# Modulation's products in other forms: whole squares of weights ahead of block 0, the condition as small operand later

## The chip, the core and the metric

The kernel runs on one core of a Trainium2 chip. The metric is the device time of one execution in microseconds (us), the median of several runs. A core has a matrix engine (TensorE, here PE, with its weight loads listed as PEld), three engines for elementwise work (VectorE or DVE, ScalarE or ACT, GpSimd or POOL) and SyncE (SP), whose queue issues nearly all of this kernel's transfers. Each engine takes its instructions strictly in the order of the program. Engines wait for each other by semaphores. SBUF is the memory on the core, with 128 partitions. PSUM holds the results of matrix products.

A matrix product takes two operands. The stationary one is loaded first (a LDWEIGHTS, with as many columns as the result has partitions). The moving one streams through it; its columns are the columns of the result. For each float32 product that the program writes the trace has two records of load and product, for a transpose one.

## The reference

One transformer block whose normalizations are modulated by a condition. x has 8 batches of 1024 tokens of 512 features, the condition 8 rows of 512:

```python
mod = jax.nn.silu(condition) @ Wada + bada
sh_a, sc_a, gt_a, sh_m, sc_m, gt_m = jnp.split(mod, 6, axis=1)
xn = _layernorm(x, g1, be1)
xm = xn * (1.0 + sc_a[:, None, :]) + sh_a[:, None, :]
x = x + gt_a[:, None, :] * _attention(xm, Wqkv, Wproj, bproj)
xn = _layernorm(x, g2, be2)
xm = xn * (1.0 + sc_m[:, None, :]) + sh_m[:, None, :]
h = jax.nn.gelu(xm @ W1 + b1, approximate=False)
x = x + gt_m[:, None, :] * (h @ W2 + b2)
```

Attention has 16 heads of 32 features and is causal. Everything is float32. The change is about the first line: the condition's product with Wada, 8 rows by 512 by 3072, in six parts of 512 columns. Parts 0 and 1 (shift and gain of attention), 3 and 4 (shift and gain of the MLP) are made by `modulation(i)`, parts 2 and 5 by `gates`.

## The kernel before, in words

**Blocks.** The tokens are cut into 16 blocks of 512 (two for each batch). For each block the kernel projects K, Q and V, computes the scores and their softmax in 4 groups of 4 heads, projects out, and runs the MLP. The linear products use a scheme with seven products of quarters in place of eight (`strassen`, which makes `product("A11", "B11")`, then S2·T2, A12·B21, S1·T1, S3·T3, and as a tail S4·B22 and A22·T4). It needs sums of quarters of the weights (S1 to S4; `weight_sums`, line 826, on POOL, at the start for k, q, v of block 0) and differences of quarters of the activations (T1 to T4; lines 784, 786 and `either`, lines 167 and 170).

**Weights.** All weights come through a ring of 8 buffers of 256 KB, "w". `fetch` (lines 358 to 362) issues the load of the next piece on SP as soon as the program has released the buffer that it needs. A matrix of 512 by 512 is read as four quarters of 256 by 256 columns; `RAW` gives their order, (0,0), (1,0), (0,1), (1,1): first the half of the rows, then the half of the columns.

**Order of work.** The instruction streams are written by a planner in the program itself. It keeps a clock for each engine (`now`), books a duration for each instruction (`note`, `note_pe`), and knows when each buffer is written and free (`written`, `left`). The linear work is a list of steps, `plan`, run as a generator that yields whenever something else could go first. Plan -1, ahead of attention, is: modulation 0 and 1, the sums for K, the columns `norm_columns_a` (lines 488 to 491: gain and shift from modT), the transposes of block 0 ("at": line 764, then the modulated activations xm_a, lines 768 and 774), K, Q and V of block 0. While it runs, `alone[0]` is True. Then `alone[0]` becomes False, and plan 0 runs beside the attention of block 0: the preparation of W1 and W2 ("preps"), K of block 1, the gates of attention, Q, modulation 3, the transposes of block 1, V, modulation 4, the MLP's columns, the gates of the MLP. Beside attention, the planner at each step takes the thread whose booked wait is shortest, and picks DVE, ACT or POOL for a copy or a sum by its booked clocks (`sooner`, `either`, `copy_out`). So a booked duration at one place can move instructions at all later places.

**The preparation.** `preparation` (lines 847 and 170 or 167, with the stores of line 816) loads every quarter of W1 and W2 into a stage, replaces them in place by S1 to S4, and stores these to memory, from where later steps load them. Its loads and stores are issued on SP, between the loads of weights.

**The products that are changed.** `cond_act` is the condition after silu, 8 rows; four transposes on PE (line 445) and a copy (line 447) turn it into `condT`, 128 partitions by 4 pieces of 8 columns. `modulation(i)` takes four quarters of Wada. For each of 4 pieces c of the result and each of 4 pieces k of the sum it calls the helper `matmul` (lines 212 to 223), which makes four products, each with 32 columns of the weights as stationary operand and the 8 columns of condT as moving one (line 217): 64 products for one modulation. Result: 128 partitions (features) by 4 by 8, in a PSUM bank. `combine_out` (line 208) adds bada's columns into `modT`. `gates` (line 520) uses condT as the stationary operand instead (8 columns) and 256 columns of Wada as the moving one.

Of the kernel before, what the change touches and what calls it, by code (L numbers as in the profile page):

```python
# [9 lines left out]
F32 = mybir.dt.float32  # L10
# [12 lines left out]
def kernel(  # L23
# [33 lines left out]
    nc = tc.nc  # L57
    B, T, D = x.shape
    HD = W1.shape[1]
    P = 128  # L60
    hd = D // H
    scale = float(hd) ** -0.5
    TB = 512
    NTT = TB // P
    NHALF = T // TB
    NC = D // P
    NF = HD // P
    HPG = P // hd
    NMOD = 6 * NC
    NQ = HD // D  # L70
    HB = D // 2
    RING = 8

    const = ctx.enter_context(tc.tile_pool(name="const", bufs=1))
# [6 lines left out]
    tmp = ctx.enter_context(tc.tile_pool(name="tmp", bufs=2))  # L81
# [18 lines left out]
    COLUMN = 0.84  # L100
# [4 lines left out]
    def due(reads=(), writes=()):  # L105
        t = 0.0
        for k in reads:
            t = max(t, written.get(k, 0.0))
        for k in writes:
            t = max(t, left.get(k, 0.0))  # L110
        return t

    def note(engine, ns, reads=(), writes=(), port=False):
        start = max(now[engine], due(reads, writes))
        if port:
            start = max([start] + [b for a, b in pool_spans if a <= start < b])
        end = start + ns
        now[engine] = end
        if engine == "POOL":
            pool_spans.append((start, end))  # L120
            del pool_spans[:-16]
        for k in reads:
            left[k] = max(left.get(k, 0.0), end + SYNC)
        for k in writes:
            written[k] = end + SYNC
        return end
# [9 lines left out]
    def note_pe(ns, form, reads=(), writes=()):  # L136
        now["PE"] = max(now["PE"], due(reads, writes))
        if shape[0] != form:
            shape[0] = form
            now["PE"] += SWITCH  # L140
        note("PE", ns, reads)
        spent[0] += ns
        for k in writes:
            written[k] = now["PE"] + PIPE

    def note_act(ns, func, reads=(), writes=()):
        if func is not None and table[0] != func:
            table[0] = func
            ns += TABLE
        note("ACT", ns, reads, writes)  # L150

    def sooner(reads, writes, dve, act):

        t = due(reads, writes)
        return "DVE" if max(now["DVE"], t) + dve <= max(now["ACT"], t) + act else "ACT"
# [18 lines left out]
    banks = [ps_l.tile([P, TB], F32, tag=f"l{i}", name=f"bank_{i}") for i in range(3)]  # L174
    live = [False] * len(banks)
    BANK = "a bank"
# [5 lines left out]
    def lin_bank():  # L182
        i = min(
            (i for i in range(3) if not live[i]),
            key=lambda i: left.get(("l", i), 0.0),
        )
        live[i] = True
        return i

    def copy_out(dst, bank, src, writes=(), last=True):  # L190

        key = ("l", bank)
        if sooner([key], writes, 690, 585) == "DVE":
            nc.vector.tensor_copy(dst, src)
            note("DVE", 690, [key], writes)
        else:
            nc.scalar.copy(dst, src)
            note_act(585, None, [key], writes)
        live[bank] = not last
# [12 lines left out]
    def matmul(ps, lhsT, rhs, start, stop, reads=(), bank=None):  # L212

        for j in range(HPG):
            r = slice(j * hd, (j + 1) * hd)
            columns = lhsT[:, r] if len(lhsT.shape) == 2 else lhsT[:, j, :]
            nc.tensor.matmul(  # L217
                ps[r, :], columns, rhs, start=start, stop=stop, skip_group_check=True
            )
        n = 1  # L220
        for d in rhs.shape[1:]:
            n *= d
        note_pe(2 * COLUMN * n, "columns", reads, [] if bank is None else [("l", bank)])
# [30 lines left out]
    for w in range(1, NB):  # L254
# [11 lines left out]
        else:  # L266
# [10 lines left out]
            at = [("at", w + 2)] if w + 2 < NB else []  # L277
# [25 lines left out]
    RAW = ((0, 0), (1, 0), (0, 1), (1, 1))  # L303
# [43 lines left out]
    def fetch():  # L347

        while len(ring) < len(order) and (len(ring) < RING or len(ring) - RING in used):
            i = len(ring)  # L350
            at = order[i]
            is_sum = isinstance(at[2], str)
            if is_sum and (id(at[0]), *at[1:]) not in kept_sums:
                return
            w = wp.tile([P, D], F32, tag="w", name=f"w_{i}")
            note_dma(680, [], [("w", i)], freed.get(i - RING, 0.0) + 300)
            if len(at) == 4:
                nc.sync.dma_start(w.rearrange("p (k n) -> p k n", n=HB), quarter(*at))
            elif is_sum:
                nc.sync.dma_start(w, kept_sums[id(at[0]), at[1], at[2]])  # L360
            else:
                nc.sync.dma_start(w, rows_of(*at))
            ring.append(w)

    def take(count):
        i = taken[0]
        taken[0] += count
        return list(range(i, taken[0]))
# [6 lines left out]
    def release(*indices):  # L375
        used.update(indices)
        for i in indices:
            freed.setdefault(i, now["PE"])
        fetch()
# [10 lines left out]
    at, r0 = [], 0  # L390
# [29 lines left out]
    ident = const.tile([P, P], F32, tag="ident", name="ident")  # L420
# [4 lines left out]
    nc.gpsimd.memset(eps, EPS)  # L425
    ones = const.tile([P, hd], F32, tag="ones", name="ones")
    nc.gpsimd.memset(ones, 1.0)
    minus_half = const.tile([P, NTT], F32, tag="minus_half", name="minus_half")
    nc.gpsimd.memset(minus_half, -0.5)
    minus_ones = const.tile([P, P], BF16, tag="minus_ones", name="minus_ones")  # L430
# [12 lines left out]
    pc = banks[0][:, : NC * B].rearrange("p (c b) -> p c b", b=B)  # L443
    for c in range(NC):
        nc.tensor.transpose(pc[:, c, :], cond_act[:, ts(c, P)], ident[:B, :B])
    condT = const.tile([P, NC, B], F32, tag="condT", name="condT")
    nc.vector.tensor_copy(condT, pc)
    pcols = banks[1][:, :n_rows]
    nc.tensor.transpose(pcols, rows, ident[:n_rows, :n_rows])
    cols = const.tile([P, n_rows], F32, tag="cols", name="cols")  # L450
    nc.vector.tensor_copy(cols, pcols)
    modT = const.tile([P, NMOD, B], F32, tag="modT", name="modT")

    def modulation(i):
        at = take(4)
        fetch()
        if len(ring) <= at[-1]:
            yield [tail_key[0]], []
        part = {kf: halves(j) for kf, j in zip(RAW, at)}
        yield [("w", i) for i in at], [BANK]  # L460
        bank = lin_bank()
        pm = banks[bank][:, : NC * B].rearrange("p (c b) -> p c b", b=B)
        for c in range(NC):
            for k in range(NC):
                w = part[k // 2, c // 2][:, k % 2, ts(c % 2, P)]
                matmul(pm[:, c, :], w, condT[:, k, :], k == 0, k == NC - 1, [("w", i) for i in at], bank)
                note("PE", 90)
                yield [], []
        release(*at)
        combine_out(  # L470
            modT[:, ts(i, NC), :],
            bank,
            pm,
            cols[:, O_BADA + i * NC : O_BADA + (i + 1) * NC].unsqueeze(2).to_broadcast([P, NC, B]),
        )

    def half(i, size):
        return slice(i * size, (i + 1) * size)
# [104 lines left out]
    alone = [True]  # L583
# [1410 lines left out]
```

## Time and profile before

| | |
|---|---|
| median of 3 runs | 3505.04 us (3502.97 to 3507.28) |
| the profiled execution, its own time | 3510.74 us |
| its span, first to last instruction | 3509.0 us |
| PE busy | 3454.3 us, 98% |
| DVE, POOL, ACT busy | 2198.9, 2084.2, 1212.4 us |
| DMA, mean rate over the span | 140 GB/s |
| granted TensorE clock | 0.998 |

A row of the timeline has the start, the duration, the engine, the line, the operation, result<-operands, shapes and a count of merged instructions. In brackets stands how long the engine had been idle before, and what ended that; "issue" means that the profile shows nothing that the engine waited for. SPq is the queue of SP: a row of it is the issue of a transfer, not the transfer. The view by windows gives each engine's busy time and number of instructions in a stretch, then the granted clock, the mean busy share of the 16 DMA engines and the rate. The view of groups gives count | busy us, mean ns | idle us before. The view of waits gives who waited <- for whom: us in total, times, the longest.

### The profile page before, as it was taken

The page shows a single profiled execution, that of the slowest core. Times are in us where ns is not written, and L with a number is a line of the kernel's source. Part 1 is how long each engine was busy: PE and PEld are TensorE (multiplying, and loading weights), DVE is VectorE, ACT ScalarE, POOL GpSimd, SP SyncE. Part 2 cuts the span into 40 slices and gives each one's busy share as a digit, 9 for nine tenths or more (in the row PEclk, how much of TensorE's full clock was granted, in tenths as well). Part 3 has the DMA queues.
Part 4 walks back from the last instruction along what each step waited for, and adds up shares of the span by engine and source line. Part 5 has one row for each costly group of instructions (what it writes and reads, how often), then busy time and mean ns, then how long its engine had stood idle before and what let it go on. Part 6 is the DMA issues. An engine that isn't in the chain of part 4 may idle for free.

```text
span 3509.0 us, 120365 instructions
## 1 busy us (share of the span) xinstructions
PE 3454.3 (98%) x54429; PEld 1724.0 (49%) x54429; DVE 2198.9 (63%) x2401; ACT 1212.4 (35%) x1276; POOL 2084.2 (59%) x2258
## 2 busy tenths in 40 slices
PE   8999999999999999999999999999999999999999
PEld 4444445445554545445454454544555444554445
DVE  5766676564666656665666566765666756656563
ACT  2335333342233423335223342333423343232531
POOL 3767846666366663756727576275753658537660
PEclk9999999999999999999999999999999999999999
DMA  6843444535545445363454534545354544443334
GB/s 212 263 137 104 137 115 140 142 107 159 142 125 156 119 147 153 119 170 115 137 157 130 155 117 144 150 137 148 116 155 137 165 122 146 128 136 101 96 121 140
DMA packets 328194, 491.10 MB, mean 140 GB/s; under 512 B 27260, under 2 KB 177596, under 8 KB 324100
## 3 DMA queue, kind: packets, MB, share of 16 engines
q1 hardware_dynamic: 327568, 483.39, 47.1%
q8 instruction: 428, 7.01, 0.8%
q14 instruction: 82, 0.67, 0.1%
q10 hardware_dynamic: 116, 0.03, 0.0%
HBM read 425.57 MB, written 55.64 MB: 137 GB/s over the span
## 4 chain that ended last, share of the span: by engine, by line
PE 83%; POOL 7%; DMA 3%; DVE 3%; ACT 1%; issue 1%; SPq 1%; ACTq 0%; DVEq 0%; POOLq 0%
PE bank L217 59%; PE sc L1595 8%; PE st L1686 6%; PE po L1726 6%; POOL pT L1816 4%; PE st L1674 2%; PE bank L1747 2%; DMA hat_m<-held_m 1%; DVE mx L1610 1%; POOL hT L170 1%; ACT pT L1698 1%; DMA held_m<-xm_m 1%; PE bank L1648 0%; POOL xr L170 0%; DMA w<-in_L_cond_Wqkv_dram 0%
## 5 line engine op out<-in xcount | busy, mean ns | idle before, releaser
L1816 POOL TENSOR_TENSOR pT<-pT,pT 128x256 f32<-128x256 f32 (+3 forms) x1254 | 1219.7, 1007 | 298.5 <-PE po L1726 181.6
L1698 ACT ACTIVATE pT<-st 128x2048 f32<-128x2048 f32 x288 | 540.9, 1878 | 1065.1 <-PE st L1686 959.8
L217 PE MATMUL bank<-w,hT 128*32 128x256 f32 x14336 | 823.7, 380 | 0.4 <-issue 0.4
L1610 DVE TENSOR_REDUCE mx<-sc 128x4 f32<-128x2048 f32 (+3 forms) x384 | 665.9, 1755 | 235.6 <-PE sc L1595 229.5
L217 PEld LDWEIGHTS bank<-w,hT 128*32 128x32 f32 x14336 | 446.7, 110 | 390.3 <-issue 105.8
L217 PE MATMUL bank<-xm_m,w 128*32 128x256 f32 x8192 | 498.6, 381 | 3.6 <-ACT xm_m L774 2.2
L217 PE MATMUL bank<-t_m,w 128*32 128x256 f32 x6144 | 382.4, 380 | 0.9 <-DVE t_m L786 0.6
L217 PEld LDWEIGHTS bank<-xm_m,w 128*32 128x32 f32 x8192 | 255.6, 110 | 231.2 <-issue 62.2
L1703 POOL TENSOR_SCALAR_AFFINE_SELECT pT<-pT 128x512 f32<-128x512 f32 x256 | 167.5, 672 | 331.9 <-ACT pT L1698 329.4
L1607 DVE TENSOR_TENSOR sc<-sc,mask 128x1024 f32<-128x1024 f32 (+1 forms) x160 | 162.8, 1018 | 293.3 <-PE sc L1595 237.8
L1595 PE MATMUL sc<-kT,qT 32*128 32x512 f32 (+3 forms) x3072 | 329.5, 521 | 4.3 <-ACT pT L1698 3.3
L1726 PE MATMUL po<-pT,v 128*32 128x512 f32 (+3 forms) x3048 | 301.6, 490 | 3.9 <-POOL pT L1703 3.9
L1686 PE MATMUL st<-qT,kT 32*128 32x512 f32 (+3 forms) x3072 | 300.8, 487 | 0.0
L217 PEld LDWEIGHTS bank<-t_m,w 128*32 128x32 f32 x6144 | 189.6, 110 | 172.9 <-issue 48.5
L1765 DVE RECIPROCAL rec<-rec 128x128 f32<-128x128 f32 x256 | 227.3, 922 | 48.2 <-ACT rec L1756 48.2
L217 PE MATMUL bank<-xm_a,w 128*32 128x256 f32 x3968 | 243.4, 382 | 0.4 <-DMA w<-in_L_cond_Wqkv_dram 0.4
L217 PE MATMUL bank<-w,qT 128*32 128x512 f32 x2048 | 237.0, 595 | 1.1 <-DMA w<-in_L_cond_Wproj_dram 0.7
L1595 PEld LDWEIGHTS sc<-kT,qT 32*128 32x128 f32 x3072 | 129.6, 183 | 188.2 <-issue 88.4
L208 DVE TENSOR_TENSOR hT<-bank,u_u 128x512 f32<-128x512 f32 x187 | 126.6, 686 | 105.8 <-PE bank L217 103.1
L217 PE MATMUL bank<-t_a,w 128*32 128x256 f32 x2944 | 183.2, 380 | 0.0
L217 PEld LDWEIGHTS bank<-xm_a,w 128*32 128x32 f32 x3968 | 123.5, 110 | 110.3 <-issue 29.3
L1115 ACT ACTIVATE hT<-hT,cols 128x512 f32<-128x512 f32 x256 | 164.7, 712 | 35.9 <-DVE hT L208 28.5
(243 smaller groups left out, 3404.0 us busy)
## 6 DMA issues: line engine op xcount, KB each, us to landing
w<-in_L_cond_W_dram SPq DMA_DIRECT2D x384, 256.0 KB
w<-kept_up_S SPq DMA_DIRECT2D x256, 256.0 KB
w<-kept_down_S SPq DMA_DIRECT2D x256, 256.0 KB
w<-kept_qkv_S SPq DMA_DIRECT2D x180, 256.0 KB
w<-in_L_cond_Wqkv_dram SPq DMA_DIRECT2D x147, 256.0 KB
hat_a<-in_x_dram SPq DMA_DIRECT2D x64, 256.0 KB
xr<-in_x_dram SPq DMA_DIRECT2D x32, 512.0 KB
w<-in_L_cond_Wproj_dram SPq DMA_DIRECT2D x64, 256.0 KB
```

Of the source, the lines that this page charges most:

```text
L208: nc.vector.tensor_tensor(out, src, other, op)
L217: nc.tensor.matmul(ps[r, :], columns, rhs, start=start, stop=stop, skip_group_check=True)
L1115: nc.scalar.activation(hT[:, i, :], hT[:, i, :], AF.Gelu, bias=cols[:, O_B1 + f : O_B1 + f + 1])
L1595: nc.tensor.matmul(sc[:, j, c0 : c0 + w], qTs[n][r, gg, ts(qt, P)], keys_of(n, kh)[r, gg, :w], start=True, stop=True, skip_group_check=True,)
L1607: nc.vector.tensor_tensor(place, place, shape_of.to_broadcast(place.shape), ALU.add)
L1610: nc.vector.tensor_reduce(maxima[n, gg][:, kh, qt, :], sc[:, :, c0 : c0 + w], axis=AX.X, op=ALU.max)
L1686: nc.tensor.matmul(st[:, j, c0 : c0 + w], kT[r, gg, ts(k % NTT, P)], qT[r, gg, TB - w :], start=False, stop=True, skip_group_check=True,)
L1698: nc.scalar.activation(pT[:, :, :used], st[:, :, :used], AF.Exp, scale=scale)
L1703: nc.gpsimd.affine_select(diagonal, diagonal, pattern=[[0, HPG], [1, P]], compare_op=ALU.is_ge, fill=0.0, base=0, channel_multiplier=-1,)
L1726: nc.tensor.matmul(po[r, TB - w :], v[:, k % NTT, g * P + j * hd : g * P + (j + 1) * hd], pT[:, j, c0 : c0 + w], start=(k == 0), stop=last ...
L1765: nc.vector.reciprocal(some, some)
L1816: nc.gpsimd.tensor_tensor(into, into, pT[:, j, c0 : c0 + w], ALU.add)
```

## The change

Three things. First, `condT` becomes the first 8 columns of each 32-column piece of `cond_cols`, whose other columns are zero, and POOL makes a matrix `folded` at the start: four identity matrices of 32 by 32 under one another. Second, while `alone[0]` is True (modulation 0 and 1), a product takes a whole square of 128 by 128 weights as stationary operand and 8 columns of condT as moving one: 16 products in place of 64. They go quarter by quarter in the order in which the quarters are loaded, and each quarter's buffer is released right after its four products. Third, beside attention (modulation 3 and 4), `cond_cols` (32 columns) is the stationary operand and 256 columns of weights move. The four pieces k of the sum go to four different groups of 32 partitions of one bank, 8 products. A copy brings the bank to SBUF (`parts`, a tile of the tag "y"), and four products with `folded` add the four groups and turn the result so that features are on partitions, as before. The planner books 220 ns for each whole product, and 430 ns for each half of the columns in the third case; before it booked 103 ns for each of 16 calls. `modT` gets 20 pieces in place of 24; the last four were never written.

```diff
+    folded = const.tile([P, hd], F32, tag="folded", name="folded")
+    for j in range(HPG):
+        nc.gpsimd.tensor_copy(folded[j * hd : (j + 1) * hd, :], ident[j * hd : (j + 1) * hd, j * hd : (j + 1) * hd])
...
-    condT = const.tile([P, NC, B], F32, tag="condT", name="condT")
+    cond_cols = const.tile([P, NC, hd], F32, tag="condT", name="condT")
+    nc.gpsimd.memset(cond_cols, 0.0)
+    condT = cond_cols[:, :, :B]
     nc.vector.tensor_copy(condT, pc)
...
-    modT = const.tile([P, NMOD, B], F32, tag="modT", name="modT")
+    modT = const.tile([P, 5 * NC, B], F32, tag="modT", name="modT")
...
         bank = lin_bank()
+        if not alone[0]:
+            for fh in range(2):
+                for k in range(NC):
+                    nc.tensor.matmul(
+                        banks[bank][ts(k, hd), half(fh, HB)], cond_cols[:, k, :], part[k // 2, fh][:, k % 2, :],
+                        start=True, stop=True, skip_group_check=True,
+                    )
+                note_pe(2 * COLUMN * HB, "columns", [], [("l", bank)])
+            release(*at)
+            parts = tmp.tile([P, TB], F32, tag="y", name=f"mod_{i}")
+            copy_out(parts, bank, banks[bank], [("mod", i)])
+            yield [("mod", i)], [BANK]
+            bank = lin_bank()
         pm = banks[bank][:, : NC * B].rearrange("p (c b) -> p c b", b=B)
-        for c in range(NC):
-            for k in range(NC):
-                w = part[k // 2, c // 2][:, k % 2, ts(c % 2, P)]
-                matmul(pm[:, c, :], w, condT[:, k, :], k == 0, k == NC - 1, [("w", i) for i in at], bank)
-                note("PE", 90)
-                yield [], []
-        release(*at)
+        if not alone[0]:
+            for c in range(NC):
+                nc.tensor.matmul(
+                    pm[:, c, :], parts[:, ts(c, P)], folded[:, :B], start=c == 0, stop=True, skip_group_check=True,
+                )
+                note_pe(220, "whole", [("mod", i)], [("l", bank)])
+        for j, (kh, fh) in enumerate(RAW if alone[0] else ()):
+            for c in range(2 * fh, 2 * fh + 2):
+                for k in range(2 * kh, 2 * kh + 2):
+                    nc.tensor.matmul(
+                        pm[:, c, :], part[kh, fh][:, k % 2, ts(c % 2, P)], condT[:, k, :],
+                        start=j + c + k == 0, stop=k == NC - 1, skip_group_check=True,
+                    )
+                    note_pe(220, "whole", [("w", at[j])], [("l", bank)])
+                    yield [], []
+            release(at[j])
```

## The prediction

> **What bounds the kernel now.** I read the page first: busy times, queues, the chain that ended last.
>
> ```profile
> PE 3454.3 (98%) x54429; PEld 1724.0 (49%) x54429; DVE 2198.9 (63%) x2401; ACT 1212.4 (35%) x1276; POOL 2084.2 (59%) x2258
> ...
> q8 instruction: 428, 7.01, 0.8%
> ...
> PE 83%; POOL 7%; DMA 3%; DVE 3%; ACT 1%; issue 1%; SPq 1%; ACTq 0%; DVEq 0%; POOLq 0%
> ```
>
> TensorE is busy for 3454.3 of 3509.0 us and holds 83% of the chain. Only two things can move the time: PE's own work, and the 55 us in which PE stands. So the second view is the busy time by windows, cut at the places that the change touches (columns: us, PE, PEld, DVE, ACT, POOL, clock, DMA share, GB/s).
>
> ```profile
> 0.00:24.20 24.20, 9.71 (x281) 8.16 (x281) 9.64 (x23) 6.66 (x9) 6.45 (x17) 1.00 0.76 234
> 24.20:100.00 75.80, 75.80 (x1221) 41.00 (x1224) 51.85 (x67) 21.39 (x25) 32.15 (x41) 1.00 0.65 204
> 100.00:150.00 50.00, 45.12 (x896) 24.39 (x888) 37.09 (x46) 13.35 (x15) 35.57 (x50) 1.00 0.91 281
> 150.00:1000.00 850.00, 834.71 (x12864) 407.24 (x12868) 548.89 (x587) 303.25 (x316) 525.63 (x584) 1.00 0.46 135
> 1000.00:3509.00 2509.00, 2488.90 (x39184) 1243.18 (x39176) 1551.46 (x1680) 867.72 (x913) 1484.38 (x1569) 1.00 0.47 136
> ```
>
> PE stands 14.5 us before 24.2, never from there to 100, 4.9 us from 100 to 150, and 35.4 us in the 3359 us after. The change works in the first stretch (modulation 0 and 1) and the third (modulation 3 and 4). In the third, DMA is the nearly full resource. The third view is PE's timeline at the start.
>
> ```profile
> 13.55 1.15 PE L217 MATMUL bank<-condT,w 128*32 128x8 f32 x64 [0.27 <-DMA w<-in_L_cond_Wada_dram]
> 15.05 0.30 PE L217 MATMUL bank<-condT,w 128*32 128x8 f32 x8 [0.35 <-DMA w<-in_L_cond_Wada_dram]
> ...
> 18.42 0.72 PE L217 MATMUL bank<-condT,w 128*32 128x8 f32 x40 [3.07 <-issue]
> 19.07 2.82 PE L764 MATMUL bank<-ident,hat_a 128*128 128x128 f32 x12
> 23.13 1.12 PE L764 MATMUL bank<-ident,hat_a 128*128 128x128 f32 x4 [1.24 <-ACT xm_a L774]
> 24.18 3.03 PE L217 MATMUL bank<-xm_a,w 128*32 128x256 f32 x32
> 27.03 1.90 PE L217 MATMUL bank<-t_a,sums_k 128*32 128x256 f32 x32
> 35.67 1.91 PE L217 MATMUL bank<-t_a,w 128*32 128x256 f32 x32
> ```
>
> The last quarter of Wada is there at 15.05. Then PE stops 3.07 us in the middle of modulation 1, with weights and condition present and no releaser but "issue".
>
> **The change, part by part.**
>
> *The stall at 15.35.* PE had run 221 records by then:
>
> ```profile
> 0.00:15.40 15.40, 5.17 (x221) 1.00 0.80 246
> ```
>
> Queue q8 moves 428 packets of 7.01 MB, 16.4 kB each; PE issues twice 54429 records (loads and products), so 254 instructions to a packet. It is PE's instruction stream, and 221 records are 442 instructions, near two packets. I read the stall as a packet that came late. Modulation 0 and 1 now are 256 records; afterwards they are 16 products each, of two records, 64 in all. Then 221 records are reached only some 136 records past the 16 transposes, in the K projection, some 7 us after its start, when the packet has had twice the time. The stall goes.
>
> The Trainium skill, "Runtime: NRT & Kernel Launch", section "Instruction fetch mechanics", speaks against this: instructions come in 16 KiB blocks of 256 that the sequencer fetches itself while it executes, and the cost of a boundary is mostly hidden. The packet size agrees with 254 here, "hidden" does not agree with 3.07 us; if it held, the stall would be something else and stay (rival three).
>
> *The products themselves.* Whole squares load 128 columns each. The nearest row in that cold first stretch is the transposing of the condition, 128 columns loaded, 8 moved:
>
> ```profile
> 6.52 0.56 PE L445 MATMUL bank<-ident,cond_act 8*128 8x8 f32 x4 [6.52 <-ACT cond_act L439]
> ```
>
> Less the 0.24 of the last one's tail that is 0.107 us a record, 0.86 for the 8 records of a quarter. This is more PE time than now (3.4 us a modulation against 2.3, twice the 1.15 of the row of 13.55), but beside the landing of Wada. Quarters now go in the order they land: the second of modulation 1 starts at about 13.7, the last ends at about 16.3. So modT is ready near 16.5. After it stand four small DVE operations:
>
> ```profile
> 19.20 0.19 DVE L208 TENSOR_TENSOR modT<-bank,cols 128x32 f32<-128x32 f32 x1 [6.13 <-PE bank L217]
> ...
> 19.64 1.22 DVE L489 TENSOR_TENSOR gaina<-onepa,cols 128x32 f32<-128x32 f32 x1
> ...
> 21.00 1.21 DVE L491 TENSOR_TENSOR shifta<-shifta,modT 128x32 f32<-128x32 f32 x1
> ```
>
> Two of them took 1.2 us while POOL worked from 19.55 on; at 16.7 POOL still waits for weights (row below), so I take 0.2 to 0.4 each, done near 17.8 instead of 22.2. What is late next: PE's transposes, 12 in 2.6 us from 16.4 and 4 in 0.85, so the first K product at about 20.0 instead of 24.18, its length 2.85 as now. The second product needs POOL's second sum, the seventh of K needs POOL's t_a after eight sums:
>
> ```profile
> 19.55 1.26 POOL L826 TENSOR_TENSOR sums_k<-w,w 128x512 f32<-128x512 f32 x1 [16.93 <-DMA w<-in_L_cond_Wqkv_dram]
> 20.89 1.26 POOL L826 TENSOR_TENSOR sums_k<-sums_k,w 128x512 f32<-128x512 f32 x1
> ...
> 30.86 1.27 POOL L170 TENSOR_TENSOR t_a<-t_a,xm_a 128x512 f32<-128x512 f32 x1
> ```
>
> The sums start when Wqkv lands, behind Wada in the same DMA queue; that stays. Second sum at 22.15, second product at 22.9 instead of 27.03; seventh at 22.9 + 5 x 1.73 = 31.5, but t_a ends at 32.1, so 32.2 instead of 35.67. **Lead at 36 us: 3.5 us** (bounds: 0 if the stall stays; 4.1 if POOL does not hold the seventh). The four added POOL copies and the memset lie in the 17 us in which POOL waits for Wqkv; without that cover they would cost under 1 us. PE has no gap until 100, so the lead arrives there whole.
>
> *Modulation 3 and 4.*
>
> ```profile
> L217 PE MATMUL bank<-condT,w 128*32 128x8 f32 x256 | 3.2, 178 | 0.0
> ```
>
> They go: 3.2 us. They are replaced by 16 products of 256 columns, at the 1.73 us that 16 such products take (27.03 to 28.76 in the K projection: 32 records), 8 whole products of two records at 0.107 at most, 1.7 us (half at the full clock), and two more changes of form and back. That is 2.6 to 3.8, so -0.6 to +0.6; I take 0. The copy between the two steps is ACT's and PE does other products meanwhile (two sums of scores, two linear products in the new order). The tile that it fills is one of the two "y" buffers, free since the gate row's store, and b_out for gates m waits for the last matrix product on SP; behind it there stand weights that PE, by its order, reaches over 15 us of products later.
>
> *What moves.* The planner books other durations (16 times 220 ns for 16 times 103 at the start), so from the first V product on its choices differ: in the new instruction order PE has 1955 changes of form against 1965, and SP, from its 48th row on, another order of the preparation's loads. A change of form costs no more than the tail of a product, 0.18 us (1.91 busy, 1.73 step); a third of it, ten times, is -0.6 us. SP's order counts more, because of the third stretch:
>
> ```profile
> 119.00:150.00 31.00, 26.90 (x512) 14.23 (x504) 22.17 (x28) 8.47 (x8) 21.78 (x33) 1.00 0.99 293
> ...
> 115.24 3.32 SPq L847 DMA_DIRECT2D prep_down<-in_L_cond_W_dram  x4
> ...
> 139.46 0.39 SPq L358 DMA_DIRECT2D w<-in_L_cond_Wada_dram  x1
> 143.03 0.34 SPq L816 DMA_DIRECT2D kept_up_S<-prep_up  x1
> 144.11 1.59 SPq L358 DMA_DIRECT2D w<-in_L_cond_Wqkv_dram  x2
> ...
> 150.47 1.03 PE L520 MATMUL bank<-w,condT 128*8 128x256 f32 x4 [1.95 <-DMA w<-in_L_cond_Wada_dram]
> 151.91 0.85 PE L217 MATMUL bank<-xm_a,w 128*32 128x256 f32 x12 [0.41 <-DMA w<-in_L_cond_Wqkv_dram]
> ```
>
> DMA is 99% busy at 293 GB/s, and PE waits for the last quarter of Wada and for Wqkv. Counted along SP's order in transfers of 256 KB, that last quarter is the 128th now and the 134th afterwards: the store of 143.03 and four loads of prep_down stand ahead of it, and one more transfer earlier. Six transfers are 1.57 MB, at 293 GB/s 5.4 us. The full stretch begins when PE frees weight buffers and sums are done, so I let it begin earlier by the lead: 5.4 - 3.5 = **+1.9 us** when PE goes on, at about 152.4. PE comes there 3.5 us early and waits some 7 us: the lead is spent. Bounds: +5.4 if the stretch begins no earlier; -3.5 if the four loads of prep_up that SP now issues after 91 us, and in the new order ahead of two weights of Q, fill its earlier gap and make up for all. Soon after that SP's count is the same within two transfers in both orders, and DMA's share falls to 0.46 (window from 150).
>
> *The sum.* +1.9 - 0.6 = +1.3 us. The profiled execution took 3510.74 (span 3509.0 and 1.7 around it), 5.7 over the median of 3505.04; it would take 3512.0. Carried to the median: **3506 us**.
>
> **The rest of the run.** All later work is the same, in another order. Where PE stands after 150 us:
>
> ```profile
> PE st L1674 <- DVE mx L1610: 7.8, 8, 2.4
> PE po L1726 <- POOL pT L1703: 3.9, 5, 1.7
> PE bank L764 <- ACT hat_m L687: 3.5, 3, 2.7
> PE bank L1648 <- POOL mcols L1632: 3.3, 4, 1.3
> ```
>
> Twenty waits in these four groups, the longest of each in the last column, each a near miss of two engines. A new order deals them anew. Independent, they scatter by about 6 us; I centre that on zero and put it into the range.
>
> **Rivals.** *One, faster:* the lead is kept (the preparation, ahead by one load, leaves room) and the dealt waits fall by 5: 3505 - 3.5 - 5 = 3496. For it: a gap of SP that the load now fills.
>
> ```profile
> 82.50 0.83 SPq L360 DMA_DIRECT2D w<-kept_qkv_S  x2
> 91.08 0.32 SPq L816 DMA_DIRECT2D kept_up_S<-prep_up  x1
> ```
>
> SP issued nothing from 83.3 to 91.1. Against: the count of transfers in the full stretch.
>
> *Two, slower:* the store that now is issued at 143.03 waits for a sum of the preparation, and in the new order the last quarter of Wada stands behind it and four loads (0.83 us each, by the row of 115.24). If that sum comes no earlier, Wada is issued at 143.03 + 0.34 + 3.3 + 0.3 = 147.0 instead of 139.46, all of the third stretch ends 7.5 us later: 3512.5, over 0.2% above. It decides if the fourth sum is done later than 139 us; nothing in the order says by how much it moved up.
>
> *Three, the change does not do what it says:* the stall at the start was no late packet, or it comes again in the K projection. Then no lead, and the six transfers cost up to 5.4: 3505 to 3510, middle 3508.
>
> **How the numbers follow.** Forecast (lead spent, waits even; own range 3500 to 3512) 0.5; rival one 0.17; two 0.25; three 0.08. Each measured to about 0.2%, 7 us, which is what a measurement can tell from no change: of the forecast I count 0.03 as faster and 0.05 as slower by the scatter, of rival two 0.05 as same, of three 0.02 as slower. Faster 0.20, same 0.53, slower 0.27. The range reaches from rival one to rival two with the scatter of the waits behind it: 3494 to 3520.
>
> **What would show it.** Right: no "issue" gap near 15 us, modT of modulation 1 near 16.5, first K product near 20, the seventh waiting for POOL's t_a; then PE waiting 5 to 8 us at the last gates product before 155 us. Wrong: a stall of 3 us inside the K projection; the last Wada in time with PE still 3 us ahead at 160; or waits after 160 us that differ from 35 us by more than 8.

## The result, and the profile after

| | before | after |
|---|---|---|
| median of 7 runs beside each other | 3507.28 us (3502.97 to 3516.64) | 3519.81 us (3515.49 to 3522.39) |
| ratio, after to before | | 1.003, interval 1.002 to 1.004 |
| the profiled execution, its own time | 3510.74 us | 3519.79 us |
| its span | 3509.0 us | 3517.9 us |

The change costs about 10 us (7 to 14 by the interval), 0.3%. The forecast was 3506, no difference to be measured, with 3520 as the upper end of its range. So the time lies just inside the range, and the sign is that of rival two, to which with the others I gave 0.27.

First the page of the kernel after: busy times, shares of the chain that ended last.

```profile
PE 3462.8 (98%) x54029; PEld 1733.8 (49%) x54029; DVE 2218.3 (63%) x2426; ACT 1213.1 (34%) x1272; POOL 2087.2 (59%) x2249
...
PE 86%; POOL 4%; DVE 4%; DMA 3%; ACT 1%; issue 1%; SPq 0%; ACTq 0%; DVEq 0%; POOLq 0%
```

PE has 400 records fewer and is busy for 8.5 us longer. Fewer instructions were not less work. Then the view by windows, cut as in the prediction.

```profile
0.00:24.20 24.20, 16.21 (x77) 16.02 (x78) 6.62 (x21) 5.21 (x7) 7.83 (x22) 1.00 0.67 211
24.20:100.00 75.80, 75.80 (x1199) 40.37 (x1201) 51.05 (x68) 21.26 (x27) 31.02 (x37) 1.00 0.68 216
100.00:150.00 50.00, 44.27 (x704) 23.74 (x700) 38.30 (x46) 16.02 (x17) 34.58 (x50) 0.98 0.84 264
150.00:1000.00 850.00, 835.74 (x12832) 408.63 (x12836) 551.32 (x587) 303.95 (x317) 527.96 (x582) 1.00 0.45 135
1000.00:3509.00 2509.00, 2485.88 (x39152) 1242.59 (x39148) 1567.03 (x1697) 866.65 (x905) 1485.79 (x1559) 1.00 0.46 136
```

Up to 24.2 us PE is busy for 16.21 us (9.71 before) and yet gets through 77 records in place of 281. From 100 to 150 the granted clock is 0.98 and DMA is less full than before (0.84, was 0.91). PE's timeline shows the start:

```profile
8.89 13.79 PE L490 MATMUL bank<-condT,w 128*128 128x8 f32 x64 [1.30 <-DMA w<-in_L_cond_Wada_dram]
...
26.28 2.78 PE L217 MATMUL bank<-xm_a,w 128*32 128x256 f32 x32
```

The issue gap of 3.07 us is gone, and so are the waits for Wada's quarters, but the 64 records now last 13.79 us, 0.213 us each, without a pause. The first K product starts at 26.28: 2.1 us later than before (24.18), not 4.2 earlier. Now the third stretch. The rows of L470 and L483 are the new forms, the others its waits and what follows them:

```profile
108.99 1.05 PE L470 MATMUL bank<-w,condT 128*32 128x256 f32 x16
...
114.63 1.06 PE L483 MATMUL bank<-folded,mod 128*128 128x8 f32 x8
...
123.17 1.93 PE L217 MATMUL bank<-w,t_a 128*32 128x256 f32 x32 [1.67 <-DMA w<-kept_qkv_S]
...
144.21 1.06 PE L483 MATMUL bank<-folded,mod 128*128 128x8 f32 x8
...
149.81 2.09 PE L1622 MATMUL sc<-kT,qT 32*128 32x512 f32 x8 [3.38 <-DVE mx L1637]
151.82 4.63 PE L547 MATMUL bank<-w,condT 128*8 128x256 f32 x15
156.08 0.42 PE L217 MATMUL bank<-xm_a,w 128*32 128x256 f32 x3
```

No row here waits for Wada. PE waits 1.67 us for weights of V and 3.38 us for DVE's reduction of the scores, and right after that the 15 records of the gates take 4.63 us. The clock in that place, by windows:

```profile
147.50:154.30 6.80, 4.50 (x14) 1.30 (x15) 4.24 (x5) 2.93 (x4) 4.83 (x9) 0.50 1.08 334
```

For 6.8 us the granted clock is 0.50; PE is busy for 4.50 of them, so up to half of that, 2.25 us, is lost (an estimate). PE reaches the first product of block 1 with xm_a at 156.08, before at 151.91. For the remainder, one window from 160 us to the end in both kernels, before and then after:

```profile
160.00:3600.00 3440.00, 3314.49 (x51916) 1645.95 (x51904) 2093.00 (x2257) 1165.65 (x1222) 2006.82 (x2150) 1.00 0.46 132
```

```profile
160.00:3600.00 3440.00, 3316.48 (x51984) 1649.76 (x51976) 2115.21 (x2284) 1167.08 (x1217) 2008.92 (x2136) 1.00 0.45 132
```

Span less 160 less busy is the time in which PE stands: 3509.0 - 160 - 3314.5 = 34.5 us before, 3517.9 - 160 - 3316.5 = 41.4 us after. So PE waits 6.9 us longer in the rest of the run, where not one product was changed, and is busy 2.0 us longer there. That is another cut than the one at block 1, where 4.2 of the span's 8.9 us are lost already and 4.7 come behind it; the 2.2 us of busy time between the two accounts I did not trace. Which waits, says PE's view of waits from 160 us on, after:

```profile
PE st L1701 <- DVE mx L1637: 10.7, 9, 2.6
...
PE bank L1774 <- POOL pT L1843: 2.4, 1, 2.4
```

The first group had 7.8 us in 8, the last 0.9.

### The profile page after: what moved, and what is told of

Read it like the earlier page. It is cut to its first block, busy times and chain, and to the rows that moved or that the text cites. A ratio compares the mean times of both kernels' runs of the same rounds, so it can differ in the third digit from the quotient of the medians.

```text
span 3517.9 us, 119581 instructions
## 1 busy us (share of the span) xinstructions
PE 3462.8 (98%) x54029; PEld 1733.8 (49%) x54029; DVE 2218.3 (63%) x2426; ACT 1213.1 (34%) x1272; POOL 2087.2 (59%) x2249
## 4 chain that ended last, share of the span: by engine, by line
PE 86%; POOL 4%; DVE 4%; DMA 3%; ACT 1%; issue 1%; SPq 0%; ACTq 0%; DVEq 0%; POOLq 0%
PE bank L217 60%; PE sc L1622 8%; PE po L1753 6%; PE st L1713 6%; PE st L1701 2%; POOL pT L1843 2%; PE bank L1774 2%; DVE mx L1637 1%; POOL hT L170 1%; DMA hat_a<-held_a 0%; ACT pT L1725 0%; DVE sc L1634 0%; PE bank L1675 0%; DMA w<-in_L_cond_Wproj_dram 0%; DMA w<-kept_qkv_S 0%
## 5 line engine op out<-in xcount | busy, mean ns | idle before, releaser
L1730 POOL TENSOR_SCALAR_AFFINE_SELECT pT<-pT 128x512 f32<-128x512 f32 x256 | 175.2, 702 | 325.3 <-ACT pT L1725 322.7
```

What stands on the lines that cost most here:

```text
L1730: nc.gpsimd.affine_select(diagonal, diagonal, pattern=[[0, HPG], [1, P]], compare_op=ALU.is_ge, fill=0.0, base=0, channel_multiplier=-1,)
```

## Experiments

The gain or loss in us is the ratio's interval times the time of before, about 3507. All the runs:

| run | what it is | median us | ratio, interval | us against before |
|---|---|---|---|---|
| e1 | before, start in whole squares | 3513.42 | 1.0016, 1.0007 to 1.0025 | +5.6 |
| e2 | first half of the change | 3515.84 | 1.0025, 1.0015 to 1.0036 | +8.8 |
| e3 | second half of the change | 3520.67 | 1.0039, 1.0026 to 1.0052 | +13.7 |
| e4 | after, start in 32 columns | 3526.39 | 1.0055, 1.0043 to 1.0068 | +19.3 |
| e5 | after, with the order of before | 3511.90 | 1.0011, 1.0002 to 1.0020 | +3.9 |
| e6 | before, with the order of after | 3512.16 | 1.0017, 1.0009 to 1.0026 | +6.0 |
| e7 | before, start in 64 columns | 3509.25 | 1.0004, 0.9995 to 1.0013 | +1.4 |
| e8 | after, start in 64 columns | 3524.29 | 1.0046, 1.0033 to 1.0058 | +16.1 |
| e9 | e7, T4 ahead of the sums for Q | 3503.45 | 0.9987, 0.9978 to 0.9995 | -4.6 |
| e10 | e5, start in 64 columns | 3513.48 | 1.0014, 1.0005 to 1.0023 | +4.9 |

The median of before beside them was 3506.73 (e1 to e4), 3507.99 (e5 to e8) and 3508.72 (e9, e10).

### The halves of the change, and the width of the start (e1 to e4)

Theory A: the new order that the planner's bookings bring costs most, and the whole squares some 2 us. Theory B: the whole squares cost most.

**e1.** Only the products ahead of block 0 become whole squares; bookings and order stay those of before.

```diff
-                matmul(pm[:, c, :], w, condT[:, k, :], k == 0, k == NC - 1, [("w", i) for i in at], bank)
+                if alone[0]:
+                    nc.tensor.matmul(
+                        pm[:, c, :], w, condT[:, k, :], start=k == 0, stop=k == NC - 1, skip_group_check=True,
+                    )
+                    note_pe(2 * COLUMN * B, "columns", [("w", i) for i in at], [("l", bank)])
+                else:
+                    matmul(pm[:, c, :], w, condT[:, k, :], k == 0, k == NC - 1, [("w", i) for i in at], bank)
```

> The kernel before, with only the products of modulation 0 and 1 made as whole squares; bookings and every other instruction's place as before. Theory A (the new order of all later work costs most of the 12.5 us; the whole squares cost about 2 us): 64 records of 0.213 us at the start, first K product near 26.3 instead of 24.2, no gap named issue near 15 us; of this 2 us part is taken back where PE waited for weights at 148 to 152 us. Total 0 to +3 us against before. Theory B (the whole squares cost most of it, because the late start pushes everything after it): +8 to +12 us.

Measured +5.6 us (2.5 to 8.8). PE's timeline of e1, start and modulation 4:

```profile
9.35 12.97 PE L467 MATMUL bank<-condT,w 128*128 128x8 f32 x60 [0.16 <-DMA w<-in_L_cond_Wada_dram]
...
25.89 1.93 PE L217 MATMUL bank<-xm_a,w 128*32 128x256 f32 x32
...
132.58 1.14 PE L217 MATMUL bank<-condT,w 128*32 128x8 f32 x104
...
400.53 0.39 PE L1680 MATMUL st<-mrow,minus_ones 32*128 32x512 bf16 x4 [3.67 <-DVE mx L1616]
```

The price of a whole square, 0.213 us a record in the kernel after, is confirmed: 12.97 us for 60 records, 0.216 each, and the first K product 1.7 us late. But the lag does not live. In the same order of instructions, the 104 records of modulation 4 start at 132.58, in before's timeline at 132.87:

```profile
132.87 1.14 PE L217 MATMUL bank<-condT,w 128*32 128x8 f32 x104
...
400.28 0.39 PE L1674 MATMUL st<-mrow,minus_ones 32*128 32x512 bf16 x4 [2.42 <-DVE mx L1610]
```

e1's time is lost at single places far behind: 3.67 us in place of 2.42 near 400, and, of the same kind, 2.65 in place of 0.47 for ACT near 1280. These are the same waits of the same instructions, longer. Neither theory had that, and the total lies between their ranges. Beside it, e1's own runs lie between 3507.13 and 3521.61 us.

**e2.** The whole first half: bookings of 220 ns, quarter by quarter, release of each quarter; modulation 3 and 4 as before.

```diff
+        for j, (kh, fh) in enumerate(RAW if alone[0] else ()):
+            for c in range(2 * fh, 2 * fh + 2):
+                for k in range(2 * kh, 2 * kh + 2):
+                    nc.tensor.matmul(
...
+                    note_pe(220, "whole", [("w", at[j])], [("l", bank)])
+                    yield [], []
+            release(at[j])
+        if not alone[0]:
+            for c in range(NC):
+                for k in range(NC):
...
```

> The first half of the change alone: whole squares with the new bookings and release by quarter; modulation 3 and 4 as before. Far fewer instructions change places than in the whole change (some 50 rows of PE's order against 1800 and more). Theory A: -1 to +4 us. Theory B: +8 to +12 us.

Measured +8.8 us (5.3 to 12.6), as theory B expected and over A's upper end. Its order of instructions moves only some 50 rows on PE. Its timeline shows half of the loss early: the first xm_a product of block 1 starts at 156.20 (before 151.91), after waits of 2.81 us for weights of V, 2.66 of issue and 1.97 for Wqkv.

**e3.** The second half alone; its order is nearly that of after.

```diff
+        if not alone[0]:
+            for fh in range(2):
+                for k in range(NC):
+                    nc.tensor.matmul(
+                        banks[bank][ts(k, hd), half(fh, HB)], cond_cols[:, k, :], part[k // 2, fh][:, k % 2, :],
...
+        for c in range(NC if alone[0] else 0):
             for k in range(NC):
                 w = part[k // 2, c // 2][:, k % 2, ts(c % 2, P)]
```

> The second half alone: modulation 3 and 4 with the condition as small operand, 0 and 1 as before. Its order of later work is nearly that of the whole change. Theory A: the start as before (gap of 3 us near 15, first K product at 24.2), and yet +6 to +11 us, which grow after 1000 us. Theory B: -2 to +2 us.

Measured +13.7 us (9.1 to 18.2), more than the whole change, with the start of before. So the whole squares are not needed for most of it, and theory B falls. But A had 11 at most, and it missed e2: the halves, 8.8 and 13.7, do not add up to the whole, 10.5.

**e4.** The kernel after, each whole square cut into four products of 32 columns again, quarter by quarter; the order is untouched.

```diff
-                    nc.tensor.matmul(
-                        pm[:, c, :], part[kh, fh][:, k % 2, ts(c % 2, P)], condT[:, k, :],
+                    for r in (slice(i * 32, (i + 1) * 32) for i in range(P // 32)):
+                        nc.tensor.matmul(
+                            pm[r, c, :], part[kh, fh][:, k % 2, ts(c % 2, P)][:, r], condT[:, k, :],
```

> The changed kernel, order and bookings untouched, with each whole square of modulation 0 and 1 split again into four products of 32 columns: 256 records at the start. If the gap near 15 us was a late packet of instructions, it comes back after about 221 records, first K product at 23.5 to 24.5. If it hung on the order of the quarters or of their release, it stays away, first K product at 20 to 21. In theory A the total stays 7 to 11 us over before; in theory B it falls to 0 to +3.

Measured +19.3 us (15.1 to 23.8), the slowest of all, though its timeline has the first K product at 20.56, 5.7 us earlier than after and 3 us earlier than I had expected:

```profile
9.33 0.62 PE L491 MATMUL bank<-condT,w 128*32 128x8 f32 x32 [0.52 <-DMA w<-in_L_cond_Wada_dram]
...
16.67 0.72 PE L491 MATMUL bank<-condT,w 128*32 128x8 f32 x40 [2.25 <-issue]
...
20.56 1.72 PE L217 MATMUL bank<-xm_a,w 128*32 128x256 f32 x28
```

```profile
0.00:16.50 16.50, 5.10 (x221) 1.00 0.82 265
```

Two things are shown. A record of 32 columns takes 0.019 us (0.62 for 32), an eleventh of the 0.213 of 128 columns: four of them, which load the same 128 columns, take 0.078. And the issue gap is back as soon as there are 256 records again, after exactly 221 of them, in another order and at another line. e3 has it after 221 as well (2.48 us). That is a place in the stream of instructions, not an operand. Where the place is reached only in the K projection (after, e7), there is no gap. That the instructions come late there fits all of this; no view shows their arrival.

### Order and products apart (e5, e6)

Theory C: the lasting new order costs most. Theory D: the products and the first 160 us cost most. The planner counts how much linear work is done and compares it with what is due (`spent`); the new products of modulation 3 and 4 book some 3 us more there, and this count stays 3 us ahead for the whole run.

**e5.** The whole change, but with the count kept as it was. From about 165 us on the instructions stand in the order of before.

```diff
                 note_pe(2 * COLUMN * HB, "columns", [], [("l", bank)])
+                spent[0] -= 2 * COLUMN * HB - 107.5
...
                 note_pe(220, "whole", [("mod", i)], [("l", bank)])
+                spent[0] -= 220
```

> The whole change, but what modulation 3 and 4 add to the count of linear work done is kept at the amount of before, so that the instruction order is again that of before from PE's row 415 on (about 165 us). Theory C (the lasting new order costs most): -1 to +4 us against before. Theory D (the products and the first 160 us cost most): +8 to +12 us. If both count, +4 to +8.

**e6.** The other corner: no product of before changed, only the count raised, which gives nearly the order of after.

```diff
                 note("PE", 90)
+                spent[0] += 0.0 if alone[0] else 95.3
                 yield [], []
```

> The kernel before with no product changed; only the planner's count of linear work done is raised by the 3 us that the change adds to it during modulation 3 and 4. The later order is then that of the whole change (some 100 rows of PE apart; 1756 rows from before). Theory C: +6 to +12 us. Theory D: -2 to +2 us. If both count, +3 to +7.

Measured: e5 +3.9 us (0.7 to 7.0), e6 +6.0 us (3.2 to 9.1); together 9.9, and the whole change has about 10.5. So both count. In this pair they add up to the whole, and by the medians the order has the larger share, though the two intervals overlap. The window from 160 us, of e5 and of e6:

```profile
160.00:3600.00 3440.00, 3316.14 (x51961) 1647.86 (x51952) 2093.32 (x2261) 1166.86 (x1223) 2009.34 (x2148) 1.00 0.44 132
```

```profile
160.00:3600.00 3440.00, 3310.21 (x51884) 1643.07 (x51878) 2114.31 (x2279) 1163.22 (x1213) 2010.29 (x2137) 1.00 0.44 132
```

With spans of 3508.3 and 3511.2, PE stands 32.2 us in e5 and 41.0 in e6. The same sum for all profiles:

| order of before | PE stands after 160, us | order of after | us |
|---|---|---|---|
| before | 34.5 | after | 41.4 |
| e1 | 40.7 | e3 | 46.7 |
| e2 | 35.5 | e4 | 44.1 |
| e5 | 32.2 | e6 | 41.0 |
| e7 | 36.1 | e8 | 44.4 |
| e9 | 34.6 | | |
| e10 | 33.9 | | |
| mean | 35.4 | mean | 43.5 |

Twelve profiles, and not one of the old order stands longer than any of the new (the nearest two, e1 and e6, are 0.3 us apart). A single row carries some 3 us of chance: before's profiled execution, 3510.74, is 3.5 us above its median, that of e7, 3506.32, is 2.9 below. The medians of the times say the same less cleanly: -4.6 to +8.8 us against before in the old order, +6.0 to +19.3 in the new. The two groups of the waits that make up most of it are in e6 too, whose products are those of before:

```profile
PE st L1675 <- DVE mx L1611: 9.9, 9, 2.4
...
PE bank L1748 <- POOL pT L1817: 2.4, 1, 2.4
```

The second of these is one instruction near 3380 us, where the sums of a late attention group wait for POOL; in the old order that wait has 0.9 us in before and 1.3 in e5. e3, e4 and e8 have the 2.4 us too, so this wait goes with the order. Others do not: the one near 400 us is 2.4 or 3.7 us in either order (2.42 in before, 3.67 in e1, 2.44 in after, 3.67 in e8).

### The start in halves of squares (e7, e8, e10)

If 128 columns take 0.213 and 32 take 0.019, what do 64 take, and does a start that is really earlier reach the end? The cut in two is the same in all three, on before (e7, below), on after (e8) and on e5 (e10):

```diff
+                    for r in (slice(0, P // 2), slice(P // 2, P)):
+                        nc.tensor.matmul(
+                            pm[r, c, :], w[:, r], condT[:, k, :], start=k == 0, stop=k == NC - 1,
+                            skip_group_check=True,
+                        )
```

> The kernel before, order and bookings untouched, with modulation 0 and 1 in products of 64 columns: 128 records at the start instead of 256. If a load of 64 float32 columns takes half of 0.213 us in the cold stretch and the two halves of the array load side by side, the products keep pace with the landing of Wada, the late packet of instructions is not needed, and the first K product starts near 20.5 instead of 24.2. If the two halves load one after the other, near 26. Total -4 to +3 us in the first case, since the lead can be lost where PE waits for weights at 116 to 152; 0 to +6 in the second, as with whole squares.

> The changed kernel, order and bookings untouched, with 64 columns in place of whole squares. First K product near 20.5 (loads side by side) or 26 (one after the other). If the 2 us of the start matter to the end, 3 to 8 us faster than the changed kernel; if the end is set by the later order and its waits, within 4 us of it.

> The whole change in the order of before (the count of linear work kept), with 64 columns in place of whole squares. Against the same with whole squares (3.9 us over before): if the 2 us lost at the start reach the end, 2 to 4 us faster, so 0 to +2 over before; if not, the same +2 to +6.

The timeline of e7:

```profile
9.49 6.80 PE L468 MATMUL bank<-condT,w 128*64 128x8 f32 x120 [0.62 <-DMA w<-in_L_cond_Wada_dram]
...
19.51 1.93 PE L217 MATMUL bank<-xm_a,w 128*32 128x256 f32 x32
...
30.94 1.93 PE L217 MATMUL bank<-t_a,sums_k 128*32 128x256 f32 x32 [3.61 <-POOL t_a L170]
...
34.41 1.91 PE L217 MATMUL bank<-t_a,w 128*32 128x256 f32 x32
```

Measured +1.4 us (-1.8 to 4.6) for e7. Now the start is what I had forecast for the whole squares: no issue gap, the first K product at 19.51 (forecast 20.0), a wait for POOL's t_a until 30.94. The forecast had put that wait at 32.2, on the seventh product; it is the fifth. Of the lead of 4.7 us 1.3 is left at the seventh product (34.41, before 35.67). e8 is at +16.1 (11.6 to 20.3) and e10 at +4.9 (1.8 to 8.1): on after and on e5, too, the earlier start brings nothing at the end. I had expected e8 within 4 us of after or faster; it is 5.6 slower.

e7 and e10 differ only in modulation 3 and 4 and their order up to 165 us: 1.4 against 4.9. What the new form costs there can be seen on DVE. Kernel after:

```profile
145.30 0.19 DVE L208 TENSOR_TENSOR modT<-bank,cols 128x32 f32<-128x32 f32 x1 [1.59 <-PE bank L483]
145.53 0.77 DVE L515 TENSOR_SCALAR onepm<-modT 128x32 f32<-128x32 f32 x1
...
147.47 2.28 DVE L1637 TENSOR_REDUCE mx<-sc 128x4 f32<-128x2048 f32 x1
```

And before:

```profile
142.91 0.19 DVE L208 TENSOR_TENSOR modT<-bank,cols 128x32 f32<-128x32 f32 x1 [0.36 <-PE bank L217]
...
144.83 2.29 DVE L1610 TENSOR_REDUCE mx<-sc 128x4 f32<-128x2048 f32 x1
```

The folding products are one step more, so modT comes at 145.30. The four operations for the MLP's columns stand in front of the reduction of the scores in DVE's queue, and PE's next scores wait for that reduction: the 3.38 us of 149.81, where before waited 0.84. In e5 and e10, in the old order, the same wait has 3.37 and 3.38 us; e6, with the old products, has none there. The products alone do not make it either: e3 has them and waits only 0.69 us, because there, as in before, the planner has put 12 records of the gates between the two products of scores, and they cover the reduction. The timeline of e3:

```profile
140.70 1.14 PE L1620 MATMUL sc<-kT,qT 32*128 32x512 f32 x8
141.77 2.76 PE L545 MATMUL bank<-w,condT 128*8 128x256 f32 x12
145.21 1.14 PE L1620 MATMUL sc<-kT,qT 32*128 32x512 f32 x8 [0.69 <-DVE mx L1635]
```

So it takes the new products and the local order that comes with the new bookings of the start.

### The lead kept (e9)

If POOL's t_a is what eats e7's lead, then it must be moved, not the start. e9 is e7 with the sums for Q behind K's step in the plan, so that POOL makes T4 of block 0 ahead of them; on PE nothing moves.

```diff
-        + [("load_xa", 1), ("sums", "q", 0), ("k", 0), ("norm_a", 1), ("q", 0)]
+        + [("load_xa", 1), ("k", 0), ("sums", "q", 0), ("norm_a", 1), ("q", 0)]
```

> As the kernel before with products of 64 columns in modulation 0 and 1, and on POOL the difference T4 for block 0 ahead of the four sums for Q instead of behind them; no other instruction changes its place. If POOL's order is what took the lead of the halves away, PE's wait of 3.6 us in the K projection goes, and the lead at 40 us is 4 to 5 us instead of 1.25. If a lead at 40 us reaches the end, 2 to 5 us faster than before; if it is spent where PE waits for weights between 116 and 152 us or in later waits, within 2 us of the halves alone.

Measured -4.6 us (-7.7 to -1.8), 3503.45 against 3508.72: faster than before, and so than after. Its timeline:

```profile
11.26 5.59 PE L468 MATMUL bank<-condT,w 128*64 128x8 f32 x96 [0.44 <-DMA w<-in_L_cond_Wada_dram]
...
20.39 2.32 PE L217 MATMUL bank<-xm_a,w 128*32 128x256 f32 x32
...
31.17 1.90 PE L217 MATMUL bank<-t_a,w 128*32 128x256 f32 x32
...
128.59 1.14 PE L217 MATMUL bank<-condT,w 128*32 128x8 f32 x104
```

The seventh product is at 31.17 (before 35.67), with no wait between it and the first, and modulation 4 at 128.59 in place of 132.87: the 4.5 us of lead are still 4.3 there, and the median has 4.6. In this one profile the first xm_a product of block 1 is at 144.38 (before 151.91), and the span is 7.6 us shorter. T4 moved alone, without the halves, was not run; PE in before has no wait between 24.2 and 100 us that it could take away.

## Where the prediction was right and where it was wrong, step by step

The time lies 0.2 us inside the range, and that is luck in the main: the sum forecast no difference, and the terms that made the 10 us are not those of rival two.

**The stall at 15.35.** Right. It went with the whole squares and with the halves, and came back at the 221st record in e3, e4 and e6. Rival three falls.

**The products themselves.** This step failed first. I priced a whole square at 0.107 us a record, by the condition's transposes. Measured at the start: 0.213 (13.79 for 64), twice that. Those transposes load the condition's 8 rows and move the identity, and show one record each, while a float32 product shows two; that each of its two records takes as long as two records of a transpose, no row of before showed, and I gave no upper bound. The eight quarters then take 13.8 us on PE beside a landing of Wada that takes about 7, so PE, not Wada, ends the step. The lead of 3.5 us at 36 became a lag of 2.1 at the first K product. With a piece of weights that is really as cheap as I assumed (64 columns, 0.057 us a record in e7, two to the square, 6.80 us in all), the working holds up to POOL's t_a; the wait for it came two products earlier than forecast, and the seventh product is at 34.41, not at 32.2.

**Modulation 3 and 4.** I took 0 with +0.6 as the upper end. By the rows of 108.99 and 114.63 the two steps of one modulation take about 1.0 us each, 3.9 in both against 3.2: +0.7. What I missed was dearer. I named the work that hides the copy on PE, but not what is queued behind modT on DVE: a reduction of 2.28 us, for which PE waits.

**What moves.** I expected +1.9 us from DMA, with PE waiting 5 to 8 us at the last gates product. That wait did not come: the gates' group has no idle time in after. But the transfers did move. SP's issues in after:

```profile
141.25 0.34 SPq L843 DMA_DIRECT2D kept_up_S<-prep_up  x1
142.17 5.00 SPq L874 DMA_DIRECT2D prep_down<-in_L_cond_W_dram  x4
148.02 0.37 SPq L358 DMA_DIRECT2D w<-in_L_cond_Wada_dram  x1
```

This is rival two's mechanism as described: the store is issued later than 139, and the last Wada at 148.02, where rival two said 147.0 (before 139.46). It set nothing, since PE was held by DVE until 149.81, and reached the last quarter's products without waiting. In e3, where the gates come earlier, the wait for Wada is there with 1.47 us. So rival two got the sign right by a cause that here was hidden. By the timelines of PE from 100 to 156 us the waits sum to the same in both kernels (5.6 before, of which 2.2 are issue; 5.7 after). Of the 4.2 us at the first xm_a product of block 1, 2.0 are the lag of the start, which arrives whole (the xm_a products of 105.51 stand at 103.48 in before). The 2.1 that are added are 0.7 of products, 0.1 of waits and some 1.3 that is left for the half clock, whose upper bound was 2.25.

**The rest of the run.** This step, "I centre that on zero", was off for the larger part of the time: 12 profiles give 35.4 us of waits for the old order and 43.5 for the new, and e6 alone +6.0 us of time. My bound (8 us about 35) held for after, 41.4, and a draw of 8 us is not far out of the scatter of 6. So the runs show that this new order is dearer, by 6.0 us of time in e6 and by 8.1 us of waits in the means; whether before's order is better than most, or this one a bad draw, two orders cannot tell.

**What stays open.** e2 (+8.8) and e1 (+5.6) cost more than e5 (+3.9), which has the same whole squares and the new products besides. e4 and e8 cost more than after though they start earlier. Part of that can be read: near 400 us they wait 3.66 and 3.67 us where after waits 2.44, and the clock is then halved for 3.4 us (from 402.4 and 405.6), which it is not in after. Over the whole run e8's granted clock is 0.995 and after's 0.997; 0.002 of 3520 us are 7 us, an estimate for a PE that is always busy. A shift of a few us lengthens or shortens waits at many places, as e1's rows show, and I cannot derive by how much. Ten fewer changes of form (-0.6) are too small to be seen in any run.

## What to carry to other kernels

Price an instruction by a row with the same operand type and the same number of records for one product, and where there is none, double the nearest row as the other bound before building a lead on it. When an order of instructions comes from booked durations, a local edit has two prices, that of the edit and that of the new order; keep the bookings and change the product, then the reverse, to have them apart. In this kernel a lead lived only when the next engine's bound was moved too: 4.7 us at the start were worth nothing that the runs could measure until two steps of POOL changed places.

## What the runs showed of the hardware that was not expected

**Narrow loads cost less than their share of the columns.** At the start of the run a record of 128 columns takes 0.213 us, of 64 columns 0.057, of 32 columns 0.019, each with 8 columns moving. For all 128 columns that is 0.213, 0.11 and 0.08 us. The Trainium skill, "TensorEngine Tiling (Array Packing)", section "Key Properties", says that different tiles load weights and multiply in parallel; the halves and the quarters agree with that, though no run here shows the overlap itself.

**The clock can be halved after waits of some 2.4 us.** A window of after that begins near the end of such a wait, one of 2.41 us that ends at 222.92 (another of 3.4 us begins at 2379.8, behind the wait of 2.56):

```profile
222.60:226.00 3.40, 3.08 (x16) 0.89 (x19) 3.11 (x4) 0.61 (x1) 3.32 (x5) 0.50 0.00 0
```

In before the same happens, round the wait of 2.41 us that ends at 218.81:

```profile
217.60:224.40 6.80, 5.59 (x26) 1.70 (x29) 5.44 (x4) 2.58 (x2) 6.65 (x8) 0.50 0.01 4
```

So a wait of 2.4 us can cost up to 1.5 to 2.8 us more, half of what PE is busy in these stretches (an estimate). Not every such wait does it: behind the 2.42 us that end at 400.28 in before and the 2.44 that end at 404.26 in after the granted clock is 1.00. The stretches last 3.4 or 6.8 us. The Trainium skill, "TensorE: Matmul & The Clock Gate", Part 1, states a free-running window of 3413 ns, and the slow clock after an idle window of that length. The lengths of 3.4 and 6.8 us agree; but here waits of 2.4 us were enough.

**Loads of 13.79 us without a pause did not bring PE to its full rate.** In after PE is busy for 13.79 us without a gap, and the next rows still run slowly: the first K product, 2.6 us from 26.28 to the next, where 1.73 is the step at full rate. The folding products, whole squares too, take 0.12 us a record (8 from 114.63 to 115.62) where those at the start take 0.213. In e1, after 12.97 us of the same loads, the first K product at 25.89 lasts 1.93, the full rate, so the rise does not come at a fixed place. The granted clock is shown as 1.00 at the start all the same; that the slow rate is the slow clock is read from the rates alone. The Trainium skill, "TensorE: Matmul & The Clock Gate", Part 1, says that about 3.4 us of activity are enough to warm up; 13.79 us of loads with 8 moving columns were not.
